# Depthwise taps on ScalarE with adding transfers, wider 5x5 weight transforms, and margins through DRAM

## The chip, the cores and the metric

The kernel runs on one core of a Trainium2 chip. The metric is the device time of one execution in microseconds (us); "before" is the median of three runs. Engines are named as the profile names them: PE is TensorE's matrix multiplication, PEld its weight loads, DVE VectorE, ACT ScalarE, POOL GpSimd, SP SyncE. A name with q behind it (POOLq) is the engine's sequencer, which issues transfers.

## The reference

One launch computes a whole network. Only its first layer is touched here:

```python
# image x: 64 x 64 pixels, 256 channels, float32
xc  = group_norm(x)
qkv = concatenate([conv1x1(xc, W1), conv3x3(xc, W3), conv5x5(xc, W5)])  # q, k, v: 3 x 256 channels
qkv = conv3x3(qkv, Wdw, groups=768)       # depthwise: nine taps, a weight per channel and tap
q, k, v = split(qkv)                      # 8 heads of 32 channels, 4096 pixels
q, k = l2_normalise(q), l2_normalise(k)
o = softmax(q @ k.T * temperature) @ v
x = x + conv1x1(o, Wproj)
# then: a two-way selective scan (Mamba) with its norms, and a layer of 8 experts
```

## The kernel before, in words

`conv_phase` computes q, k and v up to the end of the depthwise convolution, with the norms of q and k and the transposes of v. It fills about the first 600 us; attention and everything behind it follow. Order on each engine is the order in which the Python code issues: nothing is reordered. Data is float32 with channels on the 128 partitions, so 256 channels are two tiles t.

**Units.** The work is cut into twelve units, each one kind, one half of the image and one channel tile: k00, k01 (k, half 0, tiles 0 and 1), k10, k11 (half 1), then q00, v00, q01, v01, and q10, v10, q11, v11. Below, k10 means kind k, half 1, tile 0.

**Convolutions by transforms.** k and v are computed four output columns at a time by a Winograd scheme along the width. `inputs` builds transformed inputs V on DVE. `weights(kind, co, dy, r)` builds transformed weights on DVE from a raw piece r (one row dy of taps, 3 or 5 columns of 128 x 256) and stores each in a DRAM table (`uk`, `uv`) by transfers that POOL issues (L308). One such call is a "set": 6 DVE operations for k (six sets), 15 for v (ten sets), all of 128 x 256 elements. Raw pieces come by POOL-issued transfers into two buffers `wr` (L297). SP loads the transformed weights back as `u`. `feed` issues PE's products into four PSUM banks `cv` (L466; for q the 1x1 products, L458). `transform_out` takes the products in pairs: ACT copies the second into `c` (L495), DVE adds and subtracts (`plus`, L290) and combines (`madd`, L287) into `pad`, the unit's plane with margins. `sides` fills the side margins.

**The ring.** `wx`, `wo` (weights), `c`, `sq` (squares for the norms), `qo` and `vs` (outputs) share one ring `tp` of six buffers of 128 x 512. A new tile waits until the earlier tile in its buffer is done with, for a `wo` until its stores have landed.

**Depthwise.** `depthwise` works on a unit's `pad` in two blocks of rows, b = 0 and 1. In half 0 a block holds 768 elements per partition, in half 1 1280; half 0 leaves its last rows to half 1, which gets them as a margin of nine rows. Tap 0 is an ACT operation (L559) that writes the accumulator `acc`; taps 1 to 8 are DVE operations (L572) that add into it. For ten of the twelve units (all but q11 and v11) one of the 18 taps, tap 8 of b = 1, is computed by ACT into `spare` (L564) and added into `acc` by a transfer with an adding write, which POOL issues (L565). For v, `turn` transposes each block on PE as soon as it is done (L649, copies `vs` on ACT at L651, stores to `vd` by POOL). For q and k, `norm_sums` (L605, L606), `norm_inverse` (L613 to L615, L620) and `norm_apply` follow in rounds of three chunks.

**The order.** `depthwise` is a generator that yields after each DVE tap. The main loop runs over the units: the depthwise of unit n-1 (`before`) is stepped between the groups of unit n, 18 steps divided over the groups (3 for k, 4 for v, 1 for q; in the last stages ten at a time). `step_fill` puts weight sets and input transforms between them. So taps, weight sets, input transforms and output transforms of DVE lie in one queue, interleaved by hand. Under unit q00, which has one group, come in a row four v sets and all taps of k11.

**Margins between halves.** After a unit of half 0, ACT copies nine rows of `pad` into an `edge` buffer in SBUF (L807); before the unit of half 1, ACT copies them back (L769). There are four such buffers: one for each tile, shared by k and v, and one for each tile of q.

The lines of the main loop that step all this:

```python
                    for _ in range(10 if n in (len(units) - 1, len(units) - 3) else -(-18 // groups)):
                        step(before)
                    for _ in range(share[kind]):
                        step_fill()
                    feed()
                drain(main)
                drain(before)
```

Of the kernel before, what the change touches and what calls it, by code (L numbers as in the profile page):

```python
# [14 lines left out]
FP = mybir.dt.float32  # L15
# [3 lines left out]
AF = mybir.ActivationFunctionType  # L19
ALU = mybir.AluOpType  # L20
# [4 lines left out]
P = 128  # L25
H = W = 64
NT = H * W
C = 256
CT = C // P
# [153 lines left out]
def conv_phase(cx, xT, w1, w3, w5, temp, qd, kd, vd, uk, uv):  # L183
# [13 lines left out]
    nc, tc = cx.nc, cx.tc  # L197
    HR = 32
    LAG = 24
    TX = W // 4  # L200
    with ExitStack() as ctx:
        one = ctx.enter_context(tc.tile_pool(name="a_one", bufs=1))
        up = ctx.enter_context(tc.tile_pool(name="a_u", bufs=3))
        rp = ctx.enter_context(tc.tile_pool(name="a_r", bufs=1))
        late = ctx.enter_context(tc.tile_pool(name="a_late", bufs=1))
        tp = ctx.enter_context(tc.tile_pool(name="a_t", bufs=6))
# [21 lines left out]
        for pad in pads:  # L228
            nc.gpsimd.memset(pad[:, :, 0, 0], 0.0)
            nc.gpsimd.memset(pad[:, :, 5, TX - 1], 0.0)  # L230
        edges = {
            k: one.tile([P, 9, 4, TX], FP, name=f"edge{i}") for i, k in enumerate((0, 1, ("q", 0), ("q", 1)))
        }
        out_t = late.tile([P, 4 * N], FP, name="out_t")
        wq = one.tile([P, CT, C], FP, name="wq")
        for t in range(CT):
# [24 lines left out]
        for t in range(CT):  # L261
            x = tp.tile([P, 4, 32], FP, name="px", tag="t")
# [23 lines left out]
        def madd(out, x, f, y):  # L286
            nc.vector.scalar_tensor_tensor(out, x, f, y, ALU.mult, ALU.add)  # L287

        def plus(out, x, y, op=ALU.add):
            nc.vector.tensor_tensor(out, x, y, op)  # L290
# [7 lines left out]
            return r  # L298

        def weights(kind, co, dy, r):  # L300
            s = tp.tile([P, 2, C], FP, name="wx", tag="t")
            x, y = s[:, 0, :], s[:, 1, :]
            w = [r[:, i, :] for i in range(KS[kind])]

            def pair(i):
                o = tp.tile([P, 2, C], FP, name="wo", tag="t")
                return o, lambda: [
                    nc.gpsimd.dma_start(out=UD[kind][co][i + v - 1][:, dy, :], in_=o[:, v, :]) for v in range(2)  # L308
                ]

            o, store = pair(1)
            plus(x, w[0], w[2])
            if kind == "v":
                plus(y, w[1], w[3])
                plus(x, x, w[4])
            plus(o[:, 0, :], x, y if kind == "v" else w[1])
            plus(o[:, 1, :], x, y if kind == "v" else w[1], ALU.subtract)
            store()
            yield
            for i in (3, 5) if kind == "v" else (3,):  # L320
                o, store = pair(i)
                w_ = w if i == 3 else w[::-1]
                if kind == "k":
                    madd(x, w_[2], 4.0, w_[0])
                    odd = w_[1]
                else:
                    madd(x, w_[4], 4.0, w_[2])
                    madd(y, w_[3], 4.0, w_[1])
                    madd(x, x, 4.0, w_[0])
                    odd = y  # L330
                madd(o[:, 0, :], odd, 2.0, x)
                madd(o[:, 1, :], odd, -2.0, x)
                store()
                yield

# [182 lines left out]
            nc.scalar.copy(pad[:, rows, 5, 0 : TX - 1], pad[:, rows, 1, 1:TX])  # L520

        spare = late.tile([P, (H - LAG) * W // 2], FP, name="spare")
        diag = spare[:, 0 : 9 * P].rearrange("p (a b) -> p a b", b=P)

        def diagonal(ch):
# [14 lines left out]
        def depthwise(kind, half, t, pad):  # L540

            row0, n = (LAG, H - LAG) if half else (0, LAG)
            ch = {"q": 0, "k": CT, "v": 2 * CT}[kind] + t
            dst = accp.tile([P, (H - LAG) * W], FP, name="acc", tag="acc")
            shared = 16 if (kind, half, t) == units[-1] else 0
            mine = n - shared

            def piece(b, tap):
                dy, dx = divmod(tap, 3)
                m = mine // 2  # L550
                return (
                    dst[:, m * W * b : m * W * (b + 1)].rearrange("p (h w) -> p h w", w=W),
                    pad[:, m * b + dy : m * b + dy + m, dx : dx + 4, :].rearrange("p h s j -> p h (s j)"),
                    wdw[:, 9 * ch + tap : 9 * ch + tap + 1],
                )

            for b in range(2):
                o, src, w_ap = piece(b, 0)
                nc.scalar.activation(o, src, AF.Copy, scale=w_ap)  # L559
            away = (kind, half, t) not in units[-2:]  # L560
            if away:
                o, src, w_ap = piece(1, 8)
                x = spare[:, 0 : mine * W // 2]
                nc.scalar.activation(x.rearrange("p (h w) -> p h w", w=W), src, AF.Copy, scale=w_ap)  # L564
                nc.gpsimd.dma_start(out=dst[:, mine * W // 2 : mine * W], in_=x, accum_op=ALU.add)  # L565
            parts = [pcv.tile([P, N], FP, name="cv", tag="cv") for _ in range(shared // 8)]
            beside = [products(pad, mine + 8 * i, ps) for i, ps in enumerate(parts)]
            yield
            for b in range(2):
                for tap in range(1, 8 if b and away else 9):  # L570
                    o, src, w_ap = piece(b, tap)
                    nc.vector.scalar_tensor_tensor(o, src, w_ap, o, ALU.mult, ALU.add)  # L572
                    for _ in range(3 if beside else 0):
                        if beside and not step(beside[0]):
                            beside.pop(0)
                    yield
                if kind == "v":
                    m = mine * W // P // 2
                    turn(dst, t, row0 * W // P, m * b, m, ("tr", "ps2") if shared else ("tr",))
                while beside:  # L580
                    drain(beside.pop(0))
                if b == 0 and shared:
                    for i, ps in enumerate(parts):
                        nc.scalar.copy(dst[:, W * (mine + 8 * i) : W * (mine + 8 * i + 8)], ps)
                    turn(dst, t, row0 * W // P, 2 * m, shared * W // P, ("tr", "ps2"))
            if kind != "v":
                c0 = row0 // ROWS
                rows_left.extend((dst[:, N * j : N * j + N], kind, t, c0 + j) for j in range(n // ROWS))
                if not busy:
                    busy.append(None)  # L590
                    later(norm_sums)
# [75 lines left out]
        with tc.manual_schedule(engines=ORDERED):  # L667
# [96 lines left out]
            before = None  # L764
            for n, (kind, half, t) in enumerate(units):
                pad, r0 = pads[n % 2], 9 if half else 1
                edge = edges[(kind, t) if kind == "q" else t]
                if half:
                    nc.scalar.copy(pad[:, 0:9, 1:5, :], edge)  # L769
                    nc.gpsimd.memset(pad[:, HR + 9, :, :], 0.0)  # L770
                else:
                    nc.gpsimd.memset(pad[:, 0, :, :], 0.0)
                if kind == "q":
                    def evacuate():
                        for i in range(4):
                            r = r0 + 16 * (i // 2)
                            nc.scalar.copy(
                                pad[:, r : r + 16, 1 + 2 * (i % 2) : 3 + 2 * (i % 2), :],
                                product().rearrange("p (h s j) -> p h s j", s=2, j=TX),
                            )  # L780
                        sides(pad, r0)
                        yield

                    main, groups = evacuate(), 1
                else:
                    main, groups = transform_out(kind, pad, r0), len(PTS[kind]) // 2
                if n == 0:
                    feed()
                    for _ in range(6):
                        step_fill()  # L790
                for g in range(groups):
                    step(main)
                    feed()
                    tick()

                    for _ in range(12 if kind == "q" else 0):
# [6 lines that stand above are left out]
                    feed()  # L803
                drain(main)
                drain(before)
                if not half:
                    nc.scalar.copy(edge, pad[:, LAG : LAG + 9, 1:5, :])  # L807
                before = depthwise(kind, half, t, pad)
                if n == len(units) - 2:
                    diagonal(2 * CT + units[-1][2])  # L810
# [1594 lines left out]
```

## Time and profile before

| | |
|---|---|
| median of three runs (lowest, highest) | 3949.72 us (3949.47, 3956.82) |
| profiled execution | 3948.42 us |
| its span | 3946.3 us |
| mean granted clock of PE | 0.935 |
| busy over the span: PE, DVE, ACT, POOL | 89%, 84%, 67%, 50% |
| conv phase, 0 to 600 us, busy: PE, DVE, ACT, POOL | 500, 489, 158, 100 us |
| taps on DVE (L572) | 106 of 128x768, 76 of 128x1280 |

A line of a timeline gives the start in us, the time taken, the engine, line and operation, what it writes and reads, the number of instructions, and in square brackets how long the engine stood idle before it and what ended that. A line of a group gives the count, then the busy time in us and the mean of one instruction in ns, then the idle time just before such instructions with what ended most of it. A line on transfers gives the number, the KB of each and the median us from issue to landing. The shares over the whole span are averages over phases with different limits; the conv phase is read by itself.

### The profile page before, as it was taken

The numbers are of one execution on the slowest core, as the hardware profiler recorded it, in microseconds if no ns is written. First come the engines' busy times: TensorE is split into PE (matmuls) and PEld (weight loads), VectorE is DVE, ScalarE is ACT, GpSimd is POOL, SyncE is SP. The second block draws the span as 40 slices with busy tenths as digits, with TensorE's granted clock in tenths as the row PEclk, the third lists the DMA queues.
The fourth block names the chain that finished last, engine by engine and source line by source line (L and its number), as shares of the span: only waits on it lengthen the run. The fifth ranks groups of instructions, "written<-read, shape, count | busy, mean of one in ns | idle before, by whom it ended". The sixth has DMA issues, their size and how long they took to land. (4 is left out here: it accounts for less than half of the span.)

```text
span 3946.3 us, 41780 instructions
## 1 busy us (share of the span) xinstructions
PE 3495.0 (89%) x14792; PEld 1121.7 (28%) x14792; DVE 3308.5 (84%) x2391; ACT 2645.8 (67%) x4138; POOL 1955.5 (50%) x1422
## 2 busy tenths in 40 slices
PE   6779999999999999998788888889888888876898
PEld 2334432222222222222222222223222222322444
DVE  8997678888888887778999999999999999999222
ACT  1222338988898898877777778777777777775222
POOL 3121001111111111117889899898988889887000
PEclk9989999999999999998899989989988898988999
DMA  6343246665666665563334433443434345342211
GB/s 217 112 132 104 83 143 141 128 129 112 139 120 121 137 121 118 110 146 122 127 120 124 124 126 117 118 128 118 133 119 121 104 122 152 102 130 79 65 62 57
DMA packets 184186, 471.95 MB, mean 120 GB/s; under 512 B 39205, under 2 KB 48677, under 8 KB 183710
## 3 DMA queue, kind: packets, MB, share of 16 engines
q1 hardware_dynamic: 137166, 304.26, 24.9%
q0 software_dynamic: 44496, 156.53, 19.0%
q10 hardware_dynamic: 2304, 8.39, 0.6%
q8 instruction: 118, 1.93, 0.2%
q14 instruction: 102, 0.84, 0.1%
HBM read 268.17 MB, written 79.56 MB: 88 GB/s over the span
## 5 line engine op out<-in xcount | busy, mean ns | idle before, releaser
L1895 POOL TENSOR_TENSOR dbx<-dtxr,b 128x1024 f32<-128x1024 f32 x512 | 1203.1, 2359 | 194.3 <-DVE da L1908 104.4
L1908 DVE TENSOR_TENSOR_SCAN da<-da,state,dbx 128x1024 f32<-128x1024 f32 x432 | 1014.0, 2347 | 15.7 <-ACT da L1885 7.1
L1056 ACT ACTIVATE e<-sc 128x1536 f32<-128x1536 f32 x512 | 740.2, 1446 | 1.3 <-PE sc L1050 1.3
L1885 ACT ACTIVATE da<-dtr,aneg 128x512 f32<-128x512 f32 x1024 | 708.1, 692 | 32.9 <-DMA dtr<-dtd 2.4
L977 POOL DMA_DIRECT2D s<-s x222 | 194.0, 999 | 900.6 <-DVE s L969 523.3
L969 DVE TENSOR_TENSOR s<-s,e 128x2048 f32<-128x2048 f32 x256 | 586.7, 2292 | 44.1 <-ACT e L1056 20.7
L1050 PE MATMUL sc<-q,kS 32*128 32x512 f32 x4096 | 588.3, 639 | 4.6 <-ACT e L1055 3.9
L1913 DVE TENSOR_TENSOR h<-da,c 128x1024 f32<-128x1024 f32 x432 | 529.2, 1225 | 32.5 <-DVE da L1908 0.5
L987 PE MATMUL av<-e,vT 128*32 128x512 f32 x4096 | 545.4, 605 | 2.4 <-DVE o L993 2.4
L1948 PE MATMUL y<-h,sel 128*32 128x512 f32 x2048 | 377.5, 663 | 93.1 <-DVE h L1913 68.1
L466 PE MATMUL cv<-v,u 128*128 128x512 f32 x928 | 410.3, 603 | 37.8 <-DVE pad L287 13.6
L967 DVE TENSOR_TENSOR s<-e 128x2048 f32<-128x2048 f32 x128 | 293.2, 2291 | 127.5 <-ACT e L1056 110.0
L1055 ACT ACTIVATE e<-sc 128x512 f32<-128x512 f32 x512 | 305.9, 597 | 112.8 <-PE sc L1050 58.1
L1341 PE MATMUL mm<-u,win 128*128 128x512 f32 x464 | 243.9, 667 | 69.9 <-ACT z L1449 28.9
L1050 PEld LDWEIGHTS sc<-q,kS 32*128 32x128 f32 x4096 | 163.8, 183 | 430.7 <-ACT e L1055 387.6
L1939 ACT COPY state<-da 128x2 f32<-128x2 f32 x431 | 68.7, 160 | 300.9 <-DVE h L1913 297.4
L466 PEld LDWEIGHTS cv<-v,u 128*128 128x128 f32 x928 | 178.3, 193 | 267.0 <-issue 222.3
L572 DVE SCALAR_TENSOR_TENSOR acc<-pad,wdw_s,acc 128x768 f32<-128x768 f32 (+1 forms) x182 | 224.8, 1240 | 33.3 <-ACT acc L559 27.9
L1387 PE MATMUL mm<-xp,taps 128*128 128x512 f32 x480 | 213.3, 596 | 0.6 <-DVE m L1537 0.6
L1908 DVE TENSOR_TENSOR_SCAN h<-da,state,dbx 128x1024 f32<-128x1024 f32 x80 | 187.5, 2343 | 10.3 <-ACT state L1939 9.3
L987 PEld LDWEIGHTS av<-e,vT 128*32 128x32 f32 x4096 | 80.9, 108 | 390.9 <-issue 376.7
L1918 POOL TENSOR_TENSOR h<-h,c 128x1024 f32<-128x1024 f32 x80 | 188.3, 2353 | 1.0 <-ACT state L1939 1.0
(380 smaller groups left out, 3894.1 us busy)
## 6 DMA issues: line engine op xcount, KB each, us to landing
s<-s POOLq DMA_DIRECT2D x222, 512.0 KB, 6.4
dtr<-dtd SPq DMA_DIRECT2D x128, 512.0 KB
dtxr<-dtd SPq DMA_DIRECT2D x128, 512.0 KB
b<-bcd SPq DMA_DIRECT2D x64, 256.0 KB
c<-bcd SPq DMA_DIRECT2D x64, 256.0 KB
dtd<-dt SPq DMA_DIRECT2D x64, 256.0 KB
dtd<-few SPq DMA_DIRECT2D x64, 256.0 KB
u<-uv SPq DMA_DIRECT2D x24, 640.0 KB
```

What stands on the lines that cost most here:

```text
L466: nc.tensor.matmul(rows4(ps), u[:, dy, P * ci : P * ci + P], v[:, dy : dy + HR, ci, :], start=dy + ci == 0, stop=dy == k - 1 and ci == CT - 1,
L967: nc.vector.tensor_tensor(g.part, before, e, ALU.add)
L969: nc.vector.tensor_tensor(g.part, g.part, e, ALU.add)
L987: nc.tensor.matmul(g.av[32 * h : 32 * h + 32, :], vT[:, kb, P * t + 32 * h : P * t + 32 * h + 32], e[:, h, :], start=kb == 0, stop=kb == N ...
L1050: nc.tensor.matmul(sc[1][:, h - 1, :] if h else sc[0], kS[r, t, P * kb : P * kb + P], q_t[r, t, :], start=True, stop=True,)
L1055: nc.scalar.activation(e[:, 0, :], sc[0], AF.Exp)
L1056: nc.scalar.activation(e[:, 1:4, :], sc[1], AF.Exp)
L1885: nc.scalar.activation(da[:, v, :], dts[i, e, j][0][:, v, :], AF.Exp, scale=aneg[i % 2][:, a : a + 1])
L1895: nc.gpsimd.tensor_tensor(u, dts[i, e, j][1], bcs[i, k][0][:, None, :].to_broadcast([P, 2, N]), ALU.mult)
L1908: nc.vector.tensor_tensor_scan(das[n].rearrange("p v n -> p (v n)"), da.rearrange("p v n -> p (v n)"), u.rearrange("p v n -> p (v n)"), st ...
L1913: nc.vector.tensor_tensor(h, da, bcs[i, k][1][:, None, :].to_broadcast([P, 2, N]), ALU.mult)
L1948: nc.tensor.matmul(ys[i, e][32 * j : 32 * j + 32, :], cx.sel, hs[n + j // 2][:, j % 2, :], start=False, stop=k == SQ - 1,)
```

## The change

The change has three parts.

1. **Taps.** In the ten units that give a tap away, taps 7 and 8 of both blocks are now computed by ACT and added by transfers: four per unit instead of one. DVE is left with six taps per block. `aside(1)` runs at the start of the generator, `aside(0)` after b = 0's six DVE taps. Tap 7 goes through `spare`; tap 8 through a new buffer `spare2` in half 1, and through a free part of the accumulator in half 0. Both adds of a pair go into the same block. For v in these units, both blocks are transposed at the end.
2. **Weight sets of v.** The fifteen operations of 128 x 256 are replaced: a set is three operations of 128 x 256 and six of 128 x 512 that treat two columns of taps, or two transforms, at once. It takes six tiles of the ring instead of four. Sets of k keep their six operations.
3. **q's margins.** The two q edges lie in DRAM (`cx.rows`), written and read by transfers that POOL issues; the two edge buffers in SBUF and the four ACT copies for q go. k and v keep theirs.

Lines move: in the changed kernel `madd` is L286, `plus` L289, the raw load L296, the weight store L306, `c` L499, ACT's tap copy L572, the adding transfer L573 and DVE's taps L583.

```diff
@@ edges
-        edges = {
-            k: one.tile([P, 9, 4, TX], FP, name=f"edge{i}") for i, k in enumerate((0, 1, ("q", 0), ("q", 1)))
-        }
+        edges = [one.tile([P, 9, 4, TX], FP, name=f"edge{t}") for t in range(CT)]
+        q_edges = [cx.rows.tile([P, 9, 4, TX], FP, name=f"q_edge{t}", tag=f"q_edge{t}") for t in range(CT)]
@@ weights
+            def two():
+                return tp.tile([P, 2, C], FP, name="wx", tag="t")
+            def store(o, points):
+                for v, i in enumerate(points):
+                    nc.gpsimd.dma_start(out=UD[kind][co][i][:, dy, :], in_=o[:, v, :])
+            s, o = two(), two()
             if kind == "v":
-                plus(y, w[1], w[3])
-                plus(x, x, w[4])
+                plus(s, r[:, 0:2, :], r[:, 2:4, :])
+                plus(s[:, 0, :], s[:, 0, :], r[:, 4, :])
+                odd = s[:, 1, :]
...
+            plus(o[:, 0, :], s[:, 0, :], odd)
+            plus(o[:, 1, :], s[:, 0, :], odd, ALU.subtract)
+            store(o, (0, 1))
+            yield
...
+            s, odd, o = two(), two(), two()
+            madd(s, r[:, 4::-4, :], 4.0, r[:, 2:3, :].to_broadcast([P, 2, C]))
+            madd(s, s, 4.0, r[:, 0:5:4, :])
+            madd(odd, r[:, 3:0:-2, :], 4.0, r[:, 1:4:2, :])
+            yield
+            for f, points in ((2.0, (2, 4)), (-2.0, (3, 5))):
+                if f < 0:
+                    o = two()
+                madd(o, odd, f, s)
+                store(o, points)
+            yield
@@ depthwise
+        spare2 = late.tile([P, (H - LAG) * W // 2], FP, name="spare2")
...
+            def aside(b):
+                m = mine * W // 2
+                for tap, x in ((7, spare), (8, spare2 if half else dst[:, 2 * m : 3 * m])):
+                    _, src, w_ap = piece(b, tap)
+                    x = x[:, 0:m]
+                    nc.scalar.activation(x.rearrange("p (h w) -> p h w", w=W), src, AF.Copy, scale=w_ap)
+                    nc.gpsimd.dma_start(out=dst[:, m * b : m * b + m], in_=x, accum_op=ALU.add)
             if away:
-                o, src, w_ap = piece(1, 8)
-                x = spare[:, 0 : mine * W // 2]
-                nc.scalar.activation(x.rearrange("p (h w) -> p h w", w=W), src, AF.Copy, scale=w_ap)
-                nc.gpsimd.dma_start(out=dst[:, mine * W // 2 : mine * W], in_=x, accum_op=ALU.add)
+                aside(1)
...
-                for tap in range(1, 8 if b and away else 9):
+                for tap in range(1, 7 if away else 9):
...
-                if kind == "v":
-                    m = mine * W // P // 2
-                    turn(dst, t, row0 * W // P, m * b, m, ("tr", "ps2") if shared else ("tr",))
+                if away and b == 0:
+                    aside(0)
+                m = mine * W // P // 2
+                for part in (range(2) if b else ()) if away else (b,):
+                    if kind == "v":
+                        turn(dst, t, row0 * W // P, m * part, m, ("tr", "ps2") if shared else ("tr",))
@@ main loop
-                edge = edges[(kind, t) if kind == "q" else t]
+                if half and kind == "q":
+                    nc.gpsimd.dma_start(out=pad[:, 0:9, 1:5, :], in_=q_edges[t])
+                elif half:
+                    nc.scalar.copy(pad[:, 0:9, 1:5, :], edges[t])
                 if half:
-                    nc.scalar.copy(pad[:, 0:9, 1:5, :], edge)
...
-                if not half:
-                    nc.scalar.copy(edge, pad[:, LAG : LAG + 9, 1:5, :])
+                if not half and kind == "q":
+                    nc.gpsimd.dma_start(out=q_edges[t], in_=pad[:, LAG : LAG + 9, 1:5, :])
+                elif not half:
+                    nc.scalar.copy(edges[t], pad[:, LAG : LAG + 9, 1:5, :])
```

More of the change, by code (lines that the diff above doesn't have):

```diff
@@ L300, in weights @@
         def weights(kind, co, dy, r):
[L301 to L312, printed above, removed]
@@ L313, in weights @@
-            if kind == "v":
-                plus(y, w[1], w[3])
-                plus(x, x, w[4])
-            plus(o[:, 0, :], x, y if kind == "v" else w[1])
-            plus(o[:, 1, :], x, y if kind == "v" else w[1], ALU.subtract)
-            store()
-            yield
[L320 to L333, printed above, removed]
-                yield
+            def two():
+                return tp.tile([P, 2, C], FP, name="wx", tag="t")
@@ new lines, in store @@
+            def store(o, points):
+                for v, i in enumerate(points):
+                    nc.gpsimd.dma_start(out=UD[kind][co][i][:, dy, :], in_=o[:, v, :])
+            s, o = two(), two()
+            if kind == "v":
+                plus(s, r[:, 0:2, :], r[:, 2:4, :])
+                plus(s[:, 0, :], s[:, 0, :], r[:, 4, :])
+                odd = s[:, 1, :]
+            else:
+                plus(s[:, 0, :], r[:, 0, :], r[:, 2, :])
+                odd = r[:, 1, :]
+            plus(o[:, 0, :], s[:, 0, :], odd)
@@ new lines, in weights @@
+            plus(o[:, 1, :], s[:, 0, :], odd, ALU.subtract)
+            store(o, (0, 1))
+            yield
+            if kind == "k":
+                o = two()
+                madd(s[:, 0, :], r[:, 2, :], 4.0, r[:, 0, :])
+                madd(o[:, 0, :], odd, 2.0, s[:, 0, :])
+                madd(o[:, 1, :], odd, -2.0, s[:, 0, :])
+                store(o, (2, 3))
+                yield
+                return
+            s, odd, o = two(), two(), two()
+            madd(s, r[:, 4::-4, :], 4.0, r[:, 2:3, :].to_broadcast([P, 2, C]))
@@ L338, in conv_phase @@
+            madd(s, s, 4.0, r[:, 0:5:4, :])
[3 more added lines that the diff above has]
+                if f < 0:
+                    o = two()
+                madd(o, odd, f, s)
+                store(o, points)
+            yield
         V, free = {}, list(range(9))
```

## The prediction

> **What bounds the kernel now.** The edits lie in the convolution phase, the first 600 us of the span. The later phases wait for it, so a microsecond won or lost there is one of the total. I began with busy time by stretches of 50 us (columns: busy of PE, PEld, DVE, ACT, POOL with counts, then the granted clock, DMA share and GB/s).
>
> ```profile
> 100.00:150.00 50.00, 36.41 (x84) 15.38 (x83) 49.13 (x73) 9.49 (x15) 9.28 (x16) 0.86 0.37 114
> 200.00:250.00 50.00, 45.43 (x105) 19.48 (x106) 42.67 (x78) 14.01 (x21) 17.36 (x32) 0.94 0.47 158
> 250.00:300.00 50.00, 34.21 (x85) 13.11 (x84) 48.88 (x60) 10.54 (x16) 7.91 (x14) 0.83 0.34 106
> 300.00:350.00 50.00, 48.19 (x126) 20.25 (x125) 26.38 (x30) 17.17 (x29) 6.14 (x12) 1.00 0.33 112
> ```
>
> DVE is full up to 300 us; behind that PE is, and DVE has slack. So DVE time taken off pays only where PE stands still for DVE. The timeline of PE shows those places; I read it from 100 to 600 us and show the costly one (start, length, matmuls, and in brackets the idle time before and what ended it).
>
> ```profile
> 245.22 8.85 PE L466 MATMUL cv<-v,u 128*128 128x512 f32 x20 [1.20 <-ACT c L495]
> 254.00 1.13 PE L620 MATMUL ps<-rn,pick 32*128 32x512 f32 x6
> 255.06 1.05 PE L606 MATMUL ps<-sq,heads 128*32 128x512 f32 x4
> 262.23 1.92 PE L606 MATMUL ps<-sq,heads 128*32 128x512 f32 x2 [6.11 <-ACT sq L605]
> 273.82 6.60 PE L466 MATMUL cv<-v,u 128*128 128x512 f32 x10 [9.68 <-DVE out_t L290]
> ```
>
> The other gaps over 3 us end at 126.60 (13.59 long), 203.37 (14.42), 397.51 (4.75) and 572.45 (3.14). From 126.6 to 189, 203.4 to 244 and 273.8 to 392.8 PE runs on: nothing that DVE saves inside such a stretch moves its end. Prices come from the groups by shape and from the DMA issues (KB each, median us to landing).
>
> ```profile
> L572 DVE SCALAR_TENSOR_TENSOR acc<-pad,wdw_s,acc 128x1280 f32<-128x1280 f32 x76 | 117.5, 1551 | 17.7 <-ACT acc L559 15.1
> L572 DVE SCALAR_TENSOR_TENSOR acc<-pad,wdw_s,acc 128x768 f32<-128x768 f32 x106 | 107.4, 1018 | 15.6 <-ACT acc L559 12.8
> L564 ACT ACTIVATE spare<-pad,wdw_s 128x768 f32<-128x768 f32 x6 | 5.5, 921 | 0.0
> L564 ACT ACTIVATE spare<-pad,wdw_s 128x1280 f32<-128x1280 f32 x4 | 5.4, 1349 | 0.0
> L565 POOL DMA_DIRECT2D acc<-spare x10 | 8.9, 892 | 90.2 <-ACT spare L564 90.2
> ```
>
> ```profile
> uv<-wo POOLq DMA_DIRECT2D x60, 128.0 KB, 3.1
> ...
> acc<-spare POOLq DMA_DIRECT2D x4, 640.0 KB, 5.5
> ...
> acc<-spare POOLq DMA_DIRECT2D x6, 384.0 KB, 3.8
> ```
>
> **The taps.** DVE loses 18 taps of 768 and 12 of 1280 elements: 18 x 1.018 + 12 x 1.551 = 36.9 us. ACT gains 18 x 0.921 + 12 x 1.349 = 32.8 us, and is busy under half of every stretch. POOL gains 30 issues x 0.89 = 26.8 us, also beside other work. What costs is the order: of each pair the second add goes into the block that the first writes, so POOL holds it until the first has landed. Behind it on POOL stand weight stores, raw-weight loads and margin transfers; DVE's b=1 taps wait for both adds, and ACT's copies for b=0 wait until the buffers are free, with c and sq of the main unit queued behind them on ACT. So two landings lie in series (2 x 5.5 us, 2 x 3.8 in half 0) against six DVE taps (9.3 or 6.1 us).
>
> The row shows one add in 5.5 us and no pair. The Trainium skill, "DMA: Bandwidth & Descriptors", section "Two DMAs through the same engine are not ordered", says that only the completion semaphore orders a DMA behind another: that speaks against this change, since the wait can't be dropped. Were the pair to overlap, k11's chain below would be 4.7 us shorter and the sum -5.6 instead of -0.9; no run so far shows a pair.
>
> **The 5x5 transforms.** A set takes 5.72 us from first start to the next work (243.12 to 248.85), 15 operations of 256 at 0.38 apart. Those of 512 follow each other at 0.64 (1.28 for the two out_t). New set: 3 x 0.38 + 6 x 0.64 = 5.0, with start-up about 5.1: 0.6 less, ten times. The rows' durations (0.42 for 256, 0.685 for 512) leave a fixed part of 0.155 us per operation. The Trainium skill, "VectorE: DVE Perf Modes", section on the TRN2 errata, tabulates a fixed 58 cycles (0.06 us at 0.96 GHz) and itself notes that 150 cycles were measured; the row agrees with the 150, and by the table a set would win 0.36, not 0.6. A set now takes six ring buffers of tp instead of four, and that is where a wait can come; four sets in a row (the burst under k11) meet some already:
>
> ```profile
> 230.40 0.76 DVE L287 SCALAR_TENSOR_TENSOR wo<-wx 128x256 f32<-128x256 f32 x2 [1.71 <-DMA uv<-wo]
> ...
> 240.11 0.76 DVE L287 SCALAR_TENSOR_TENSOR wo<-wx 128x256 f32<-128x256 f32 x2 [2.83 <-DMA uv<-wo]
> ```
>
> **q's margins.** Four ACT copies of 0.665 us go, four transfers on POOL come. The reads land well ahead (their users come 9 us later or more): 0, bounds 0 and +1.
>
> Now the path, stage by stage, in the trace's times.
>
> **To 126.6:** three sets are won before PE resumes, 3 x 0.6, and a little waiting: -2.2 us.
>
> **126.6 to 203.4:** six taps of 768 go (6.2 us), but the out_t at 163 waits for ACT's c, and c for PE: the saving becomes DVE idle time. The shift stays -2.2.
>
> **203.4 to 275, unit k11 and the burst of four v sets.** k10's three taps go, -4.7 (3 x 1.55), so the burst starts at 219.53 - 2.2 - 4.7 = 212.6. Before it took 29.3 us, 22.9 of work and 6.4 of waits for stores and loads. Three of six ring buffers hold squares until about 234, so a set's outputs must wait for the stores of its earlier outputs: set 1 5.1 + one landing 3.1, set 2 5.1 + 3.1 + 4.2 (beside a raw-weight load; such stores took up to 5.3), set 3 5.1, 3.1 for the last load, set 4 5.1: 33.9 us. That ends at 246.5 instead of 248.85. (No waits at all: 20.6 us; the nearer row is the stores' 3.1.) The six taps of b=0 end at 255.8. The first add goes out after the last store, 248.3, lands 253.8; the second lands 259.4. Only then can ACT fill the second buffer again (1.35) and copy c (0.56): PE, idle since 244.02 - 2.2 = 241.8, resumes at 261.4, not at 245.2. Its 20 matmuls take 8.85 plus 2.1 (after a long idle 40 of them took 19.47 us, against 17.33 in a steady run), the sums 2.1 and 0.5: 274.9. DVE's taps are through at 259.4 + 9.3 = 268.7, so out_t (c at 272.4) is ready. Before, PE resumed at 273.82 and lost the 2.1 after that: 275.9. Net **-1.0 us**; bounds -7 (burst with little more than its old waits) and +3 (landings of 6.6, the longest shown).
>
> **392.8 to 397.5:** three taps fewer on DVE ahead of pad, but each piece runs beside work that stays; the gap of 4.75 shrinks to 3.4: **-1.4**, bounds -2.5 and 0.
>
> **Bursts under v units.** v00's and v01's adds land at about 333 and 424 with the transposes due at 341 and 429: hidden, though the whole turn of b=0 (PE's transposes, ACT's vs copies, POOL's vd stores) now comes behind b=1's taps. q10's second add would hold c by 13 us, which the four product banks absorb: 0. v10: adds at 498.7, landing 504.2, 509.7; the last copy (1.35, and some 1.4 of ACT's work ahead of it) lets the last add go at 512.5 and land at 518.2. The transposes began at 514.74 and took 3.1 and 3.6: they end at 524.9 instead of 523.36, **+1.5**, bounds 0 and +4.
>
> **Sum:** -1.0 - 1.4 + 1.5 = -0.9 us. The profiled execution took 3948.42 (2.1 around its span), so 3947.5; the median of the runs lies 1.3 above it: 3948.8 us. With all bounds -9.5 to +7. About 0.2%, 7.9 us, is what a measurement of this kernel can tell from no change; most of this lies within. Of 43 us less DVE work hardly one reaches the end: it falls where PE is the limit, or a landing takes its place.
>
> **Rivals.** *Faster: the waits do not come.* If the burst takes its old waits only (27 us, 7 earlier) and adds land in 4.9 us (the median over both sizes; 1.2 over the pair), k11's place gives -9.2, the gap at 392.8 -2.5, v10 0: -11.7, 3938 us; with no wait in the burst at all 3932. For it: PE stood idle for 17 us there, and DVE's work before it falls by 9 us. Against: the stores' waits on uv<-wo are in the trace already with four buffers per set.
>
> *Slower: the adds slow one another.* Four times as many read-modify transfers share the engines with weight loads. Each microsecond per add counts twice at k11 and three times at v10. It decides from 1.8 us more (7.3 a landing: 9 - 0.9 = 8.1); at 8.5 us it is +15 - 0.9 = +14, 3963 us. For it: the longest landing shown is 6.6, a raw-weight load of the same 640 KB takes 6.8. Against: the DMA share is a third in these stretches.
>
> *It doesn't do what it says:* if the wide, strided operations ran at twice the price of narrow ones, the sets win nothing: +2, inside the forecast's range.
>
> **Chances.** Forecast (gains off the path or eaten) 0.42; faster 0.30; slower 0.28. Own range of the forecast 3942 to 3957; over all 3934 to 3963, leaving a tenth on each side.
>
> **What would show it.** Right: DVE taps x152 at unchanged means; four v sets from about 212 to 246 with idle before them ended by uv<-wo; PE idle some 20 us up to about 261, ended by ACT c; adds landing near 5.5; transposes of v10 from about 518; PE unbroken from 275 to 390. Wrong: a burst under 28 us, or adds that overlap (faster); landings over 7 us, or a PE gap in the stretches that are unbroken now (slower).

## The result and the profile after

The changed kernel takes 3959.77 us (median of 22 runs, 3946.68 to 3965.97) against 3950.54 (22 runs of the kernel before on the same chips, 3943.47 to 3956.82): ratio 1.002, 95% interval 1.0014 to 1.0026. It is slower by about 8 us where 0.9 us less was forecast. The profiled execution took 3950.96 us with a span of 3949.1, so it lies below the median of its runs. Attention, with everything behind it, starts 9.9 us later in it, and that is near the difference of the medians; the phases behind took 7 us less in this execution than in the one of before, and their code is the same.

PE's timeline of the changed kernel, at the places where PE stands still (columns as before), with attention's first product as the last line; the same line of before starts at 597.22.

```profile
126.70 17.76 PE L470 MATMUL cv<-v,u 128*128 128x512 f32 x36 [11.84 <-DVE pad L286]
203.26 6.71 PE L462 MATMUL cv<-xpad,wq 128*128 128x512 f32 x8 [14.42 <-DVE pad L286]
263.40 10.81 PE L470 MATMUL cv<-v,u 128*128 128x512 f32 x20 [17.91 <-ACT c L499]
397.43 3.49 PE L462 MATMUL cv<-xpad,wq 128*128 128x512 f32 x4 [2.97 <-DVE pad L286]
463.75 17.43 PE L470 MATMUL cv<-v,u 128*128 128x512 f32 x40 [1.73 <-ACT c L499]
524.63 1.08 PE L663 MATMUL ps<-ident,acc 128*128 128x128 f32 x4 [6.33 <-DMA acc<-spare]
607.16 1.12 PE L1068 MATMUL sc<-q,kS 32*128 32x512 f32 x2
```

Up to 397 the two kernels are level: 126.70 against 126.60, 203.26 against 203.37, 397.43 against 397.51. The last two gaps are new. One ends with ACT's c under q10's taps, one with an adding transfer under v10's.

The groups of the changed kernel: 152 taps on DVE at the old means; ACT's copies and POOL's issues as counted; but ACT now stands 66.7 us before the larger copies, waiting for a buffer that an add still reads.

```profile
L583 DVE SCALAR_TENSOR_TENSOR acc<-pad,wdw_s,acc 128x1280 f32<-128x1280 f32 x64 | 99.1, 1551 | 37.7 <-DMA acc<-spare 19.5 <-ACT acc L564 16.1
L583 DVE SCALAR_TENSOR_TENSOR acc<-pad,wdw_s,acc 128x768 f32<-128x768 f32 x88 | 89.2, 1018 | 28.0 <-ACT acc L564 17.6 <-DMA acc<-acc 8.1
L572 ACT ACTIVATE spare<-pad,wdw_s 128x1280 f32<-128x1280 f32 x16 | 21.2, 1354 | 66.7 <-DMA acc<-spare 66.7
```

Transfers: the median of the larger adds is 5.5 us, as in the row that the sum took. The second fence is from the answer for line 573, all 40 adds. Its maximum is what the forecast missed.

```profile
acc<-spare POOLq DMA_DIRECT2D x16, 640.0 KB, 5.5
uv<-wx POOLq DMA_DIRECT2D x60, 128.0 KB, 3.0
```

```profile
DMA to landing us min/median/max: 3.7/5.0/10.2
```

Where they are is seen in POOL's timeline of the changed kernel, first q10's four adds, then v10's (the brackets give how long POOL stood idle before the add; what is queued behind it on POOL waits as well).

```profile
444.88 0.88 POOL L573 DMA_DIRECT2D acc<-spare  x1 [3.11 <-ACT spare L572]
453.51 0.87 POOL L573 DMA_DIRECT2D acc<-spare  x1 [7.74 <-issue]
454.71 0.85 POOL L573 DMA_DIRECT2D acc<-spare  x1 [0.33 <-ACT spare L572]
465.43 0.85 POOL L573 DMA_DIRECT2D acc<-spare  x1 [9.88 <-DMA acc<-spare]
...
502.22 0.89 POOL L573 DMA_DIRECT2D acc<-spare  x1 [5.11 <-ACT spare L572]
507.82 0.88 POOL L573 DMA_DIRECT2D acc<-spare  x1 [4.71 <-issue]
509.47 0.86 POOL L573 DMA_DIRECT2D acc<-spare  x1 [0.78 <-DVE acc L583]
518.99 0.86 POOL L573 DMA_DIRECT2D acc<-spare  x1 [8.66 <-DMA acc<-spare]
```

Under q10 and v10 the third add goes out 1.2 to 1.7 us after the second: another block, so nothing orders the two, and they run together. Under v10 the first took 5.1 us, the second 6.8 and the third 9.0; the fourth, which must wait for the third, left at 518.99 and landed at 524.50. The transposes of v10, due at 518.3, waited for it. DVE's six taps of b = 1, which wait for the second add, ended only 0.3 us sooner, at 524.24, so two waits end there at almost the same time:

```profile
514.69 9.55 DVE L583 SCALAR_TENSOR_TENSOR acc<-pad,wdw_s,acc 128x1280 f32<-128x1280 f32 x6 [5.76 <-DMA acc<-spare]
```

Under q10 the four adds took 8.1, 8.3, 10.2 and 5.9 us.

Busy time by stretches, the two that hold q10's and v10's adds: in the second, before had 45.35 us of PE at clock 0.93 and a DMA share of 0.32.

```profile
450.00:500.00 50.00, 48.27 (x122) 20.02 (x121) 22.00 (x26) 19.66 (x28) 5.27 (x8) 1.00 0.47 121
500.00:550.00 50.00, 40.51 (x100) 18.61 (x99) 27.54 (x21) 17.61 (x27) 8.05 (x13) 0.83 0.52 142
```

### The profile page after: what moved, and what is told of

Same layout as the page of the kernel before. It is cut to its first block, busy times and chain, and to the rows that moved or that the text cites. A ratio compares the mean times of both kernels' runs of the same rounds, so it can differ in the third digit from the quotient of the medians.

```text
span 3949.1 us, 41763 instructions
## 1 busy us (share of the span) xinstructions
PE 3480.9 (88%) x14792; PEld 1121.1 (28%) x14792; DVE 3267.8 (83%) x2301; ACT 2674.7 (68%) x4164; POOL 1986.3 (50%) x1456
## 5 line engine op out<-in xcount | busy, mean ns | idle before, releaser
L1966 PE MATMUL y<-h,sel 128*32 128x512 f32 x2048 | 368.7, 656 | 95.1 <-DVE h L1931 69.7
L583 DVE SCALAR_TENSOR_TENSOR acc<-pad,wdw_s,acc 128x768 f32<-128x768 f32 (+1 forms) x152 | 188.4, 1242 | 65.7 <-ACT acc L564 33.7
```

The costliest lines, as they stand in the source:

```text
L1966: nc.tensor.matmul(ys[i, e][32 * j : 32 * j + 32, :], cx.sel, hs[n + j // 2][:, j % 2, :], start=False, stop=k == SQ - 1,)
```

## The experiments

Times of one operation in the single profiled executions; each is the same operation in every kernel, found by its order. Between kernels that share the code, those before 130 us differ by up to 3 us, mostly from waits for raw weights. "Steps 4, 3" are the steps per group for units of k and of v. "Ratio" is against the kernel before, with its interval.

| kernel | k01's last pad | k11's | v01's | v10's | v10's first vs | first sc | ratio |
|---|---|---|---|---|---|---|---|
| before | 125.86 | 202.63 | 396.78 | 477.74 | 515.43 | 597.22 | |
| changed | 125.96 | 202.52 | 396.69 | 481.23 | 525.75 | 607.16 | 1.002 (1.0014, 1.0026) |
| 1: q10, v10 one tap | 125.70 | 203.19 | 398.50 | 480.93 | 518.62 | 601.64 | 0.9998 (0.9988, 1.0007) |
| 11: v10 one tap | 127.68 | 205.17 | 400.33 | 484.40 | 522.09 | 603.89 | 1.0001 (0.9991, 1.0011) |
| 5: as 1, steps 4, 3 | 120.39 | 193.03 | 384.60 | 475.37 | 513.06 | 595.12 | 0.9981 (0.9971, 0.999) |
| 9: as 1, steps 4, 4 | 119.31 | 191.14 | 384.79 | 464.12 | 501.81 | 583.45 | 0.995 (0.9936, 0.9964) |
| 12: before, steps 4, 4 | 120.49 | 194.78 | 387.49 | 468.76 | 506.45 | 586.84 | 0.998 (0.9969, 0.9992) |

**First: q10 and v10 with one tap away.**

```diff
             away = (kind, half, t) not in units[-2:]
+            single = away and (half and kind != "k")
-  for tap, x in ((7, spare), (8, ...)):
+  for tap, x in ((7, spare), (8, ...)) if not single else ((8, spare),):
-  for tap in range(1, 7 if away else 9):
+  for tap in range(1, (8 if b else 9) if single else 7 if away else 9):
   # aside(0) and the late turn only where away and not single
```

> The changed kernel, with units q10 and v10 back on the old scheme: one tap away (tap 8 of b = 1, one adding transfer), v10 transposed block by block; all else as changed. Theory A (series of adding transfers under q10 and v10): in the changed kernel four adds of 640 KB take 26.5 us under q10 and 22.3 us under v10, and PE loses 2.6 and 6.5 us there; both go, so the first sc matmul of attention, 607.16 us in the changed kernel and 597.22 before, comes at about 598, and the median falls by about 9 us, to the one before within 3 us. Rival B (the loss is spread: four times the adding traffic, the ring of weight tiles and the margins through DRAM slow the whole phase): sc stays at 604 or later and the median at 6 us or more above before.

The total went back to that of before, as theory A says. From v01's pad to the first sc the changed kernel loses 10.0 us against before (210.47 against 200.44) and this one 2.7; of these, 1.7 come with a low clock under q10 (see q10's term below). Its sc at 601.64 is later than the 598 expected: this execution came to v01's pad 1.8 us later than the changed kernel's.

**Second: the wide sets alone**, put into the kernel before.

> The kernel before with the new weights function alone; taps and margins as before. Theory A (six ring tiles per set make stores the limit in the burst of four v sets): the burst, 29.3 us before, takes 33 to 34 us, ACT's c after it comes later than 245, PE resumes some 4 us later than 273.8, and the first sc matmul comes at 599 to 601 instead of 597.22; total 2 to 4 us up. Rival B (the 0.6 us per set is won): burst 27 us, sc at 595 to 597, total 0 to 2 us down.

Burst 30.3 us (217.38 to 247.66), sc at 597.70, ratio 1.0008 (0.9998 to 1.0017): neither theory. Started 16.9 us after k11's last pad, as in before (12.1 in the changed kernel), the wide sets cost the burst 1 us, not 4; against before no difference is shown.

**Third: the changed kernel with the old sets.**

> The changed kernel with the old weights function: taps by ScalarE and adds, margins through DRAM, narrow 5x5 sets with four ring tiles. Theory A: the burst takes about 29 us instead of 34.0, PE resumes under k11 near 259 instead of 263.4, and some of that lasts, while q10 and v10 still lose 9 us: sc at 603 to 606 (607.16 in the changed kernel), total about 3 us below the changed kernel. Rival B (the sets cost nothing on the path, the whole loss is in the adds): sc at 607 to 608.

sc at 603.38, in A's range, but not by the sets alone. PE resumed 4.4 us later at the first gap (a raw load was waited for 3.89 us), the burst took 30.6 us, and PE resumed under k11 at 266.32, not near 259. At v01's pad, 398.81, this execution was still 2.1 us behind the changed kernel's. It won 2.3 us from there to v10's pad, where q10 cost it less, and 3.3 us behind v10's first vs, where PE's clock read 1.00 (582 to 602) against 0.87 in the changed kernel (583 to 603). Ratio 1.0013 (1.0004 to 1.0023), not apart from the changed kernel's. With the early start the ring does decide the burst, 30.6 against 34.0 us. v10's loss stays (525.31 - 481.10 is 44.21 us from its pad to its first vs, against 37.69 in before). Here DVE's taps of b = 1, and not the last add, ended PE's wait:

```profile
524.19 1.09 PE L658 MATMUL ps<-ident,acc 128*128 128x128 f32 x4 [6.03 <-DVE acc L578]
```

**Fourth: the buffers swapped for b = 0.**

```diff
-  for tap, x in ((7, spare), (8, spare2 if half else ...)):
+  for tap, x in ((7, spare), (8, spare2 if half else ...))[:: 1 if b or not half else -1]:
```

> The changed kernel with the two buffers of half 1 used in the other order for b = 0 (tap 7 through spare2, tap 8 through spare): the third add of a unit can then only go out when the second has landed, so two adds of 640 KB are never under way at once. Theory A (the transfer engines serve adds at a fixed rate; two at once take as long as two in series): each add lands in 5 to 6 us instead of up to 10.2, but the chain of four under v10 still ends within 2 us of 524.5, and sc stays at 606 to 609. Rival C (overlap itself is wasteful): the chain ends 3 us or more earlier, sc at 604. Rival D (other traffic, the loads of u, sets the 8 to 10 us): landings of 8 to 10 us remain and the chain ends near 530, sc at 612.

This kernel was executed once, for its profile, so it has no ratio. With no two adds of 640 KB of one unit together, all 40 land within 7.1 us (line 573 of this kernel): q10's in 5.2, 6.0, 5.8 and 5.9, v10's in 5.1, 6.8, 6.8 and 5.0.

```profile
DMA to landing us min/median/max: 3.7/5.0/7.1
```

So two adds at once are part of what made 8 to 10 us; they are not enough for it. Under k11 of the changed kernel two adds ran together with no weight load beside them, and landed in 5.0 and 6.1 us (the second fence, of these two), both within 8.3 us; in the third kernel two such took 8.1.

```profile
256.40 0.88 POOL L573 DMA_DIRECT2D acc<-spare  x1 [5.00 <-issue]
258.60 0.86 POOL L573 DMA_DIRECT2D acc<-spare  x1 [1.31 <-issue]
```

```profile
DMA to landing us min/median/max: 5.0/5.5/6.1
```

Under q10 and v10 a load of 640 KB of transformed weights, issued by SP at 453.5 and 508.7, ran beside the two adds, which took 11.4 and 10.6 us together. So rival D has a part in it.

Under q10, c went out 4.6 us earlier, PE's gap there is gone, and from v01's pad to v10's this kernel loses 1.3 us against before where the changed kernel loses 3.6; the swap need not be the reason (see q10's term below). Under v10 the chain ended at 524.22, within 2 us, and sc came at 607.77, both as A says, but the chain had begun 4.4 us earlier: it took 26.4 us instead of 22.3, and PE's gap grew.

```profile
524.36 1.08 PE L663 MATMUL ps<-ident,acc 128*128 128x128 f32 x4 [10.51 <-DMA acc<-spare]
```

Running two together is thus not wasteful (C falls): in the changed kernel v10's second and third took 10.6 us together (507.82 to 518.44), here 6.8 and 6.8 one after the other, and the chain of four became 4 us longer. A's fixed rate is not shown either.

**Eleventh: v10 alone with one tap** (the first experiment's edit, for v10 only).

> The changed kernel with v10 alone on the old scheme (one tap away, transposed block by block); q10 keeps its four taps. Theory A (v10's transposes wait for the last of four adds in series): sc 6 to 7 us earlier than in the changed kernel, so at 599 to 602 if the earlier stages fall as they did there, total 5 to 7 us below the changed kernel. Rival B (the first kernel's gain came from q10, or from both by half): sc at 603 or later.

The total is level with before, 1.0001, against 1.002: 7.5 us of the loss, give or take some 4 by the intervals, go with v10's four adds. In the profile v10 costs nothing any more (477.74 to 515.43 is 37.69 us in before, 37.69 here, 44.52 in the changed kernel); sc at 603.89 lies in B's range as it stands, but this execution was already 3.6 us late at v01's pad; from there to sc it took 203.56 us, against 210.47 in the changed kernel and 200.44 in before. q10 keeps a gap of 1.29 us.

**Eighth: the margins alone**, q's margins through DRAM in the kernel before.

> The kernel before with q's margins through DRAM alone. Theory A: the reads land 9 us or more ahead of their users, sc at 597 (within 1.5 us, prologue aside), total unchanged. Rival B (the transfers' 1152 rows of 256 bytes delay the loads of u or hold POOL's queue): PE gaps appear under q10 or q11, sc 2 us or more later.

sc at 598.31, ratio 1.0 (0.999 to 1.001), no new gap: theory A.

**Fifth: steps spread over the groups**, on top of the first kernel.

```diff
- for _ in range(10 if n in (...) else -(-18 // groups)):
+ for _ in range(10 if n in (...) else -(-(18 if n == len(units) - 2 else 12) // groups)):
```

> The kernel of the first experiment (q10 and v10 with one tap away) with the depthwise generator stepped 12 instead of 18 times over the groups of a unit, so 4 taps per group of k instead of 5 or 6; the taps saved now leave the earlier groups too. Theory A (the prediction's -2.2 us did not come because the steps were still handed out for 18: the saved taps fell out of the last group, where PE is the limit): the PE gaps that end at 126.6 and 203.3 shrink, PE resumes near 123.5 and 194 to 197, sc at 593 to 598, total 4 to 9 us below before. Rival B (the gaps depend on raw loads and stores, not on taps): 126.6 and 203.3 stay within 1.5 us, sc at 599 to 602, total as before.

PE resumed at 121.13 and 193.77: theory A, and more than expected, since the steps moved taps behind the gaps, besides the ones saved. At v01's pad it was 12.2 us ahead; then one leftover tap of q01, queued on DVE behind three input transforms, held ACT's copies of q10's products:

```profile
398.26 27.97 PE L470 MATMUL cv<-v,u 128*128 128x512 f32 x60 [8.15 <-ACT pad L794]
```

**Sixth: the fifth with old sets.**

> As the fifth, with the old weights function (narrow sets, four ring tiles). Theory A (with an early start the wide sets fill the ring and the burst of four v sets takes 34 to 35 us, with narrow sets 30.6): burst end 3 to 5 us sooner than in the fifth kernel relative to its start, while ten sets cost 0.6 us more each, three of them before 126: sc within 3 us of the fifth, either side, nearer -1. Rival B (ring tiles do not matter): sc 2 us later than in the fifth.

sc at 594.74 (595.12 in the fifth), ratio 0.9984 (0.9976 to 0.9993): sc as theory A says, but not its reason. The bursts took 29.8 us with wide sets (211.32 to 241.14) and 28.2 with narrow (214.40 to 242.59): in the fifth the burst starts 18.3 us after k11's last pad, not early. Wide or narrow, the sets decide nothing here.

**Seventh: the fifth with k11's pair on b = 1 alone.**

> As the fifth, and unit k11 gives away its two taps on b = 1 alone (DVE 8 + 6 taps; no adds for b = 0). Theory A (under k11 the copies for b = 0 hold ACT's c until the second add of b = 1 has landed): c comes right after the burst instead of 14 us after it, DVE does not stall between the blocks, taps end 0.7 us earlier or so, and PE's gap of 18 us splits in two as before; sc 1 to 3 us earlier than in the fifth. Rival B (DVE's taps are what PE waits for there, in whatever form): sc within 1 us of the fifth.

c came at 238.74 instead of 255.05, and PE's gap of 20.87 us split in two of 6.28 and 9.61. The profile shows sc at 590.08, the runs a ratio of 0.999 (0.9981 to 0.9999), not below the fifth's. Inconclusive by itself.

**Ninth: 4 steps per group for v as well.**

```diff
- else -(-18 // groups)):
+ else (4 if groups > 1 else 18)):
```

> As the fifth kernel (q10 and v10 with one tap away, steps spread), but 4 steps per group for v units as well as for k. In the fifth, with 3 per group, the last tap of q01 came after three input transforms, at 396.4 us, and ACT's copies of q10's products and PE behind them waited 8.15 us for it: it had been 12.2 us ahead of before at 384.6 and was 2.6 ahead at 397.6. Theory A (what the saved taps win is real, and was given back there by order alone): the gap before 398 shrinks under 3 us, the first sc matmul comes at 586 to 592 (597.22 before, 595.11 in the fifth), total 8 to 13 us below before. Rival B (something else is late there): gap of 6 us or more, sc at 594 to 596.

Theory A, and more than it asked: the gap before q10's products is 0.77 us, PE then runs on, and sc comes at 583.45.

```profile
385.53 3.70 PE L462 MATMUL cv<-xpad,wq 128*128 128x512 f32 x8 [0.77 <-DVE pad L286]
```

3928.2 us (five runs) against 3946.26, ratio 0.995: faster than both kernels.

**Tenth: the ninth with k11's pair on b = 1 alone.**

> As the ninth, with k11's pair on b = 1 alone, as in the seventh. Theory A: c under k11 not held, sc 1 to 3 us earlier than in the ninth. Rival B: within 1 us of the ninth.

sc at 588.34, 4.9 us later (3.3 of it there before k01's pad), ratio 0.9972 (0.9961 to 0.9984). The gap under k11, 20.50 us in the ninth, became two of 5.56 and 9.52, so theory A's mechanism is there, but neither pair of kernels shows a gain in the runs. Whether the tenth is slower than the ninth is not sure, as the intervals overlap a little, and why it would be stays open.

**Twelfth: the kernel before with the ninth's steps.**

> The kernel before with the stepping of the ninth alone: 4 steps per group instead of 6 (k) and 5 (v); 15 taps per unit on DVE, narrow sets, margins in SBUF. Theory A (the ninth kernel's gain needs the saved taps; stepping later alone only shifts DVE work behind a gap, to be late at the next one): the gaps that end at 126.6 and 203.4 shrink by 3 to 5 us each, and the leftover of four taps at the end of each unit gives most of it back, with a gap before 398 as in the fifth kernel: sc at 592 to 600 (597.22 before, 583.45 in the ninth), total within 5 us of before. Rival B (the order of steps is the whole gain and the saved taps are worth nothing): sc at 583 to 588, total 12 us or more below before.

Neither theory: sc at 586.84 lies in B's range, but the total, 0.998, some 8 us, is more than A allowed and less than B asked. There are only short gaps before q10's products (1.58 and 1.68 us). In the runs the order of steps alone is less than half of the ninth's gain, and the intervals (0.9969 to 0.9992, 0.9936 to 0.9964) do not meet: by the ratios some 12 us come only with what the change saves, with q10 and v10 left alone. The two profiles show 3.4 of these at the first sc; where the rest lies they do not show.

## Why the prediction was wrong, point by point

**The step that failed is v10's term**, "+1.5, bounds 0 and +4". It let the third add go at about its time and every add land in 5.5 us, so that the chain from the first add to the last landing took 19.5 us (498.7 to 518.2). Measured: 22.3 us (502.22 to 524.50), as the second took 6.8 us and the third, running beside it, 9.0, and the fourth had to wait for the third. The start at 502.22 instead of 498.7 came with the stage. The term also let the transposes win back 1.9 us, because the two blocks now follow each other: 6.7 us where before took 8.6 with its pause. They took 8.8 (524.63 to 533.39): fours of transposes took 1.08 to 1.12 us, against 0.66 for the first ones of before, with a clock that read 0.50 in that stretch and 0.82 in before's. So the stage lost 6.8 us up to its first vs (44.52 against 37.69) and 6.5 by the end of the transposes. The eleventh kernel shows the term's weight in the total. The chain (adds in a row ahead of the transposes) was named rightly; the price of one add was taken from a row in which no two adds ran together.

**q10's term**, "0, absorbed by the four product banks". c was held 21 us (463.14 against 442.14), not 13, since the first two adds took 8.1 and 8.3 us instead of 5.5 each; the banks ran dry and PE stood 1.73 us. The 60 products before that took 27.61 us where a steady run takes 25.91, with a clock of 0.83 from 430 to 440, where before had 1.00. Together some 3.5 us.

The two parts come together in the kernels. In the changed one a weight load, which waits for PE's products, came 10.5 us after the start of these products (434.41), in the very moment of the first add, 444.88:

```profile
444.88 8.92 SPq L448 DMA_DIRECT2D u<-in_w  x2
```

The eleventh has the same: clock 0.83, load at 448.51, add at 448.52, landing in 8.5 us, a gap. In the third and fourth the clock read 1.00 there, the load came 8.8 us after the start and 1.7 us ahead of the add, which landed in 5.3 and 5.2 us, and PE ran all 100 products in 43.08 us without a gap, with four adds under q10 all the same. The first kernel, with one add under q10, lost the 1.7 us as well (100 products in 44.78 us), and its add took 8.6. So q10's adds need not cost these 3.5 us; what lowered the clock there stays open.

**To 126.6**, "-2.2": +0.1. The sets were won as worked out (120.84 to 125.96 is 5.12 us, 5.1 was written). But DVE waited 2.42 and 1.47 us for raw loads where it had waited 1.07 and 0.80, and the start was 0.6 us later. Such waits differ from kernel to kernel with the same code there, so the size is uncertain; the term took a set's gain as if nothing but DVE stood behind it. The taps saved in k00 could not help, since the generator still handed out 18 steps: they fell out of the last group, behind the gap. The fifth kernel, with fewer steps per group, resumed there at 121.13.

**k11 and the burst** held in nearly every number: 33.9 us forecast, 34.0 measured (214.58 to 248.58); end of the burst 246.5, measured 248.58, later by the 2.0 us by which it started late; PE resuming at 261.4, measured 263.40 after a gap of 17.91; DVE's stall between the blocks 3.46. (Stores beside a raw-weight load took up to 7.3 us in before, not up to 5.3 as the sum says; its 4.2 did no harm.) PE's run of 40 products begins at 276.20 at full clock, where the sum had 274.9.

**The gap at 397.5**, "-1.4": the gap shrank to 2.97 us, but PE came later to it; net -0.1.

**The rival that came true** is the slower one, by its own mechanism, adds that share the engines with one another and with weight loads, at v10. Its condition, 7.3 us a landing, was met under q10 (8.1 on average), under v10 only by the third add (6.6 on average); its other place, k11, stayed at 5.0 to 6.1. It got 0.28. What spoke for it was in view: the longest landing of before, 6.6 us, was q10's, and that add had a weight load beside it.

**Sum.** Predicted at v01's pad -2.4, measured -0.1; q10 0 against +3.5; v10 +1.5 against +6.8, the rest, -0.3, behind it; -0.9 against +9.9 in the profile and +8 in the runs.

**The skill beside the trace.** "DMA: Bandwidth & Descriptors", section "Issuing engines are not separate DMA queues", says that all transfers run on the same 16 engines and interleave, whoever issued them. The trace agrees: POOL's second and third add of v10, with SP's weight load beside them, took 6.8 and 9.0 us, and the shortest add of that size 5.0. The prediction used the neighbouring section, on order, for the pair inside one block, and priced the pair that nothing orders as if it were alone.

## What to carry to other kernels

A transfer that stands in for an engine's operation brings its landing into the chain: before moving work to adding transfers, count how many must land in a row before the next user, and price those that run beside each other and beside a load above the row of one alone (here 6.8 to 10.2 us against 5.0). Leave the short ends of the pipeline (here the unit whose transposes come at once) on the engine. And when operations are taken from a hand-written order, give the steps out anew, or the saving falls out where nobody waits for it; here leaving two units alone and giving out the steps anew turned 8 us lost into 18 won, of which the new steps by themselves bring some 8.

## What the runs showed of the hardware that was not expected

Adding transfers of 640 KB from SBUF to SBUF took 5.0 us at the least. Two at once with no weight load beside them took 8.3 us for both (k11 of the changed kernel) and 8.1 (the third), less than two in a row; with a load of 640 KB beside them 10.6 and 11.4. One add took 8.1 to 8.6 us where a load left in the same moment (q10 of the changed, the eleventh and the first kernel), and 5.2 and 5.3 where the load had left 1.7 us earlier. Those of 384 KB: 3.8 us when quiet, up to 7.4. The margins of 288 KB in runs of 256 bytes took 3.2 and 5.8 us to DRAM and 3.9 and 6.2 back. The first four transposes after the gap of 6.33 us took 1.08 us, the later fours 1.11 and 1.12, against 0.66 for the first four in before.
